# Linear attention with a mixture of experts: the last product of a block inverse gets a stationary operand of 128 columns in place of 64

## The chip, the cores and the metric

The kernel runs on one core of one Trainium2 chip. A core has TensorE (matrix products, from SBUF into PSUM), VectorE, ScalarE and GpSimd (the profile's DVE, ACT and POOL), and SyncE (SP), which here issues most of the transfers. The metric is the device time of one execution in microseconds. The runs of the kernel before have a median of 4116.69 us (4110.34, 4116.69 and 4119.83).

## The reference

The input x is 2 sequences of 2048 tokens with 512 features. It is normalised, and two branches are added to x: a gated delta-rule attention with 16 heads of 128, and a mixture of 16 experts (four per token) on 512 tokens. Cut to what matters, the attention is a recurrence over time with one 128 x 128 state per head:

```python
q, k, v = (silu(conv(x @ W)) for W in (Wq, Wk, Wv))   # k also times DK ** -0.5
for t in range(T):
    err = S @ k[t] - v[t]
    S = alpha[t] * S - beta[t] * outer(err, k[t])
    o[t] = S @ q[t]
out = (layernorm(o) * sigmoid(x @ Wg)) @ Wo
```

## The kernel before, in words

All data are fp32, and an fp32 product stands in the profile as two passes (two MATMUL records and two weight loads, LDWEIGHTS); a transpose is one pass. The kernel does not step through time: it takes chunks of C = 128 tokens. Inside a chunk the recurrence is a triangular system, and its inverse is needed for each head. Heads are taken in pairs (HG = 2), so there are 8 pairs x 2 sequences x 16 chunks = 256 chunk steps. Blocks of four chunks (BLK = 512 tokens) share one projection.

The inverse of a 128 x 128 triangular matrix is put together in steps. GpSimd inverts the diagonal blocks of 32 for a whole pair (`inverses`, L201 to L232). Then, chunk by chunk, `before` (L548 to L616) doubles twice: from 32 to 64 and from 64 to 128. A doubling needs two products in a row, the off-diagonal block times one inverse, then the other inverse times that. Both heads of a pair are handled in one product, since the stationary operands hold the two heads on the diagonal, 64 rows and columns each.

- First doubling: L564 (stationary `a32`, moving `ilo`, 32 columns), a VectorE copy to `xs` (L567), L594 (stationary `ihi`, moving `xs`), from which VectorE makes `iT` (L596) and `top` (L597).
- Second doubling: L605 (stationary `a64`, moving `top[:, 0:64]`, 64 columns, both heads one below the other), a VectorE copy of 64 columns to `xs2` (L607), and L613: stationary `xs2` (128 rows, 64 columns), moving `bot` (128 columns). Its output has 64 rows and, side by side, 64 columns for each head. ScalarE copies it into the upper right part of `inv` (L614).

`after` (L618 to L683) uses it one step later: L633 (stationary `kt`, moving the state S), VectorE makes `r` (L637), L643 (stationary `inv`, moving `r`), ScalarE copies `w` (L646), L652 makes the new state, L666 and L669 the output. `output` transposes it (L699) and stores it.

`recurrence` (L708 on) mixes six ticks of these with work for later: the projections of the next block (`proj`, L151, 512 moving columns, eight passes for one output), the keys and their products for the pair after the next (L151 and L192), the experts (L966, L978, L992), and near the end of each sequence the output projection (L820). So TensorE's queue has wide projection products between the small products of a chunk, and these give the other engines time for the copies in between. On top of this, the framework schedules the recorded program with estimates of its own and sets the order of each engine's queue; a longer copy or a different product can shift it.

Constants come in one transfer at the start (L57): eight 128 x 128 matrices side by side, one of which (`K_ROW`) only holds the row number. `route` uses one column of it (L912 and L916). [...] the small products of `before` use three in turn (tag `l`, always a whole bank).

Of the kernel before, what the change touches and what calls it, by code (L numbers as in the profile page):

```python
# [7 lines left out]
F32 = mybir.dt.float32  # L8
I32 = mybir.dt.int32
AF = mybir.ActivationFunctionType  # L10
ALU = mybir.AluOpType
# [3 lines left out]
P = 128  # L15
NB, T, HID = 2, 2048, 512
H, D, KS = 16, 128, 4
C = 128
# [15 lines left out]
DW = C + 1  # L34


K_ID, K_LE, K_LT, K_GT, K_ONE, K_NEG, K_COL, K_ROW = range(8)
N_CONST = 8


@with_exitstack
def block_kernel(ctx, tc, x, wq, wk, wv, wg, wo, wa, wb, ba, bb, par, consts,
                 topk_idx, topk_w, ew0, ew1, ew2, ewd0, ewd1, out):
    nc = tc.nc
    cp = ctx.enter_context(tc.tile_pool(name="const", bufs=1))
    dp = ctx.enter_context(tc.tile_pool(name="spill", bufs=1, space=DRAM))
    ps_p = ctx.enter_context(tc.tile_pool(name="ps_p", bufs=2, space=PSUM))
    ps_l = ctx.enter_context(tc.tile_pool(name="ps_l", bufs=3, space=PSUM))
# [3 lines left out]
    def bank(pool, tag):  # L52
        return pool.tile([P, 512], F32, tag=tag, name=tag)


    cst = cp.tile([P, N_CONST, P], F32)
    nc.sync.dma_start(out=cst, in_=consts.rearrange("p (n j) -> p n j", j=P))  # L57
    ident = cst[:, K_ID, :]

    def over(m, *dims):  # L60
# [35 lines left out]
    tw = cp.tile([P, FC * TOPK], F32)  # L96
    pos = cp.tile([P, FC * TOPK], I32)

    wrow = cp.tile([P, NT], I32)
    trow = cp.tile([P, NT], I32)  # L100
# [255 lines left out]
    with ExitStack() as es:  # L356
# [135 lines left out]
        mp = es.enter_context(tc.tile_pool(name="moe", bufs=2))  # L492
# [27 lines left out]
        for i, _ in enumerate(f0):  # L520
            next(ot, None)
            next(ot, None)
            if i == 18:
                route(nc, bank, ps_l, mp, cst, topk_idx, topk_w, tw, pos, wrow, trow)
            if i in (24, 26, 28, 30):
                next(p0)
        drain(ot)
# [2 lines left out]
    def bcast(a, n):  # L530
        return bass.AP(a.tensor, a.offset, [*a.ap, (0, n)])

    def v3(t):
        return t.rearrange("p (h j) -> p h j", h=HG)

    HW = HG * D

# [2 lines left out]
    k2 = ctx.enter_context(tc.tile_pool(name="chunk", bufs=2, reuse_waits="tile"))  # L540
# [7 lines left out]
    def before(n, c):  # L548

        u, blk = blocks[n]  # L550
        b = u // NP
        hs = slice((u % NP) * HG, (u % NP) * HG + HG)
        decs, kt, op, qt, _, vs, _ = have[n]
        ci, cs = blk * CB + c, slice(c * C, (c + 1) * C)

        inv = invs[(n * CB + c) % len(invs)]
        for g in range(2):
            nc.sync.dma_start(
                out=inv[g * Q:(g + 1) * Q, :, g * Q:(g + 1) * Q],
                in_=X_d[u][1, :, g, ci, :].rearrange("h (j i) -> j h i", i=Q))  # L560


        px = bank(ps_l, "l")
        nc.tensor.matmul(px[:, 0:Q], lhsT=op["a32"][:, c, :], rhs=op["ilo"][:, c, :],  # L564
                         start=True, stop=True)
        xs = k2.tile([P, Q], F32, tag="xs", name="xs")
        nc.vector.tensor_copy(xs, px[:, 0:Q])  # L567

        pk = bank(ps_l, "l")
        for h in range(HG):  # L570
            nc.tensor.matmul(pk[:, h * C:(h + 1) * C], lhsT=kt[:, h, cs], rhs=qt[:, h, cs],  # L571
                             start=True, stop=True)
        pT = k2.tile([P, HG, C], F32, tag="pT", name="pT", bufs=3)
        for h in range(HG):
            nc.vector.scalar_tensor_tensor(
                pT[:, h, :], pk[:, h * C:(h + 1) * C], D ** -0.5, decs[h][:, c, 1:],
                ALU.mult, ALU.mult)
        yield

        pkv = bank(ps_l, "l")  # L580
        for h in range(HG):
            nc.tensor.transpose(pkv[:, h * D:(h + 1) * D], kt[:, h, cs], ident)
            nc.tensor.transpose(pkv[:, HW + h * D:HW + (h + 1) * D], vs[h][:, cs], ident)  # L583
        kv = k2.tile([P, 2, HG, D], F32, tag="kv", name="kv")
        nc.scalar.copy(kv.rearrange("p s h j -> p (s h j)"), pkv)  # L585
        kg = k2.tile([P, HG, D], F32, tag="kg", name="kg", bufs=3)
        nc.gpsimd.tensor_tensor(kg, kv[:, 0], bcast(gd1[b][:, ci, hs], D), ALU.mult)  # L587
        mark["kg"] = kg[:, 0, 0:1]
        yield
        top, bot = op["top"][:, c, :], op["bot"][:, c, :]  # L590


        pz = bank(ps_l, "l")
        nc.tensor.matmul(pz[:, 0:Q], lhsT=op["ihi"][:, c, :], rhs=xs, start=True, stop=True)  # L594
        iT = k2.tile([P, Q], F32, tag="iT", name="iT")
        nc.vector.transpose(iT, pz[:, 0:Q])  # L596
        nc.vector.scalar_tensor_tensor(  # L597
            top[:, 0:Q], pz[:, 0:Q], second[:, 0:1], top[:, 2 * Q:], ALU.mult, ALU.add)
        for h in range(HG):
            r = 64 * h  # L600
            nc.scalar.copy(bot[r:r + Q, r + Q:r + 2 * Q], iT[r:r + Q])
            nc.gpsimd.tensor_copy(inv[0:Q, h, Q:2 * Q], iT[r + Q:r + 2 * Q])  # L602
        yield
        px = bank(ps_l, "l")
        nc.tensor.matmul(px[:, 0:64], lhsT=op["a64"][:, c, :], rhs=top[:, 0:64], start=True, stop=True)  # L605
        xs = k2.tile([P, 64], F32, tag="xs2", name="xs2")
        nc.vector.tensor_copy(xs, px[:, 0:64])  # L607
        for h in range(HG):
            r = slice(64 * h, 64 * h + 64)
            nc.scalar.copy(inv[64:C, h, 64:C], bot[r, r])  # L610
        yield
        pz = bank(ps_l, "l")
        nc.tensor.matmul(pz[0:64, 0:C], lhsT=xs, rhs=bot, start=True, stop=True)  # L613
        nc.scalar.copy(inv[0:64, :, 64:C], v3(pz[0:64, 0:C]))  # L614
        yield
        found[n, c] = (pT, kv, kg, inv)  # L616

    def after(n, c):  # L618
# [23 lines left out]
        for h in range(HG):  # L642
            nc.tensor.matmul(pw[:, h * D:(h + 1) * D], lhsT=inv[:, h, :], rhs=r[:, h, :],  # L643
                             start=True, stop=True)
        w = k2.tile([P, HG, D], F32, tag="w", name="w")
        nc.scalar.copy(w, v3(pw[:, 0:HW]))  # L646
        mark["w"] = w[:, 0, 0:1]
        yield
# [6 lines left out]
        if S is None:  # L655
            nc.vector.tensor_copy(S2, v3(pss[:, 0:HW]))
        else:
            for h in range(HG):
                nc.vector.scalar_tensor_tensor(
                    S2[:, h, :], S[:, h, :], gtot[b][:, ci, h0 + h:h0 + h + 1],  # L660
                    pss[:, h * D:(h + 1) * D], ALU.mult, ALU.add)
# [46 lines left out]
    def recurrence(b, first):  # L708
# [20 lines left out]
        inv = None  # L729
        for m, at in enumerate([*steps, None, None]):  # L730
            a = before(*at) if at else none
            z = after(*steps[m - 1]) if 0 < m <= len(steps) else none
            y = output(*steps[m - 2]) if m > 1 else none
# [110 lines left out]
    recurrence(1, first)  # L844


def route(nc, bank, ps, mp, cst, topk_idx, topk_w, tw, pos, wrow, trow):

# [2 lines left out]
    n = FC * TOPK  # L853

    def small(tag, cols, dt=F32):
        return mp.tile([P, cols], dt, tag=tag, name=tag, bufs=1)
# [3 lines left out]
                      in_=topk_idx.rearrange("(c p) k -> p c k", p=P))  # L860
    nc.sync.dma_start(out=tw.rearrange("p (c k) -> p c k", c=FC),
                      in_=topk_w.rearrange("(c p) k -> p c k", p=P))
# [11 lines left out]
    for i in range(1, n):  # L874
        nc.tensor.matmul(pr[:, i * NE:n * NE], lhsT=cst[:, K_ONE, :], rhs=sel[:, 0:(n - i) * NE],
                         start=False, stop=i == n - 1)
    pc = bank(ps, "l")
    for i in range(n):
        nc.tensor.matmul(pc[:, 0:NE], lhsT=cst[:, K_ONE, :], rhs=sel[:, i * NE:(i + 1) * NE],
                         start=i == 0, stop=i == n - 1)  # L880
# [26 lines left out]
    te = small("te", NT)  # L907
# [1 line left out]
    for e in range(NE):  # L909
        nc.vector.scalar_tensor_tensor(te, cst[:, K_COL, 0:NT], ends[:, e:e + 1], te, ALU.is_ge, ALU.add)  # L910
    nc.vector.tensor_scalar(te, te, float(NE - 1), float(P), ALU.min, ALU.mult)
    nc.vector.tensor_scalar(te, te, cst[:, K_ROW, 0:1], None, ALU.add)  # L912
    nc.vector.tensor_copy(wrow, te)
    tokf = small("tokf", FC)
    for c in range(FC):
        nc.vector.tensor_scalar(tokf[:, c:c + 1], cst[:, K_ROW, 0:1], float(c * P), None, ALU.add)  # L916


    first = small("first", NT + 1)
# [82 lines left out]
def _constants():  # L1002
    import numpy as np

    i = np.arange(P)
    row, col = i[:, None], i[None, :]
    m = np.zeros((N_CONST, P, P), np.float32)
    m[K_ID] = row == col
    m[K_LE] = row <= col
    m[K_LT] = row < col  # L1010
    m[K_GT] = row > col
    m[K_ONE] = 1.0
    m[K_COL] = col
    m[K_ROW] = row
    m[K_NEG] = np.where(row <= col, 0.0, -1e30)
    return np.ascontiguousarray(m.transpose(1, 0, 2)).reshape(P, N_CONST * P)


def _expert_weights(f):
# [40 lines left out]
```

## Time and profile before

| | |
|---|---|
| median of 3 runs | 4116.69 us |
| profiled execution | 4114.8 us |
| its span, from the first to the last instruction | 4113.0 us |
| mean granted TensorE clock | 0.985 |
| TensorE busy / its weight loads | 3961.7 / 2523.9 us |
| VectorE / ScalarE / GpSimd busy | 2299.5 / 1629.9 / 1841.5 us |
| moved by DMA | 553.79 MB, mean 135 GB/s |

The profile lists one execution. "PE" is TensorE's products, "PEld" its weight loads, which lie beside them. In a group of instructions one reads the line, the engine, the operation, the names of output and inputs, the rows and columns of the stationary operand for TensorE ("128*64"), the shapes and the count; then the busy time in us, the mean duration of one in ns, and the idle time just before them with what ended it. Products on TensorE are pipelined: a record lasts longer than the distance to the next one's start, and the ends are modelled, so distances between starts tell what a product takes. The granted clock is below full in parts of the first 300 us and between the two sequences, where the page's row falls to 8 tenths at the start, and at 9 tenths or more otherwise.

### The profile page before, as it was taken

How to read it: one execution, taken by the hardware profiler on the slowest of the kernel's cores; microseconds unless marked ns; L12 is line 12 of the kernel's file. 1: busy time of each engine (PE TensorE's matmuls, PEld its weight loads, DVE VectorE, ACT ScalarE, POOL GpSimd, SP SyncE). 2: the span in 40 equal slices, each digit the busy share in tenths (PEclk: the TensorE clock that was granted, in tenths of full speed). 3: DMA queues.
4: the chain of work that ended last, by engine and by line, in shares of the span. 5: the costliest groups of instructions: out<-in, count | busy, mean ns of one | idle time of the engine just before them, and what ended most of it. 6: DMA issues, size and time to landing. Idle time of an engine off the chain costs nothing.

```text
span 4113.0 us, 60869 instructions
## 1 busy us (share of the span) xinstructions
PE 3961.7 (96%) x18684; PEld 2523.9 (61%) x18684; DVE 2299.5 (56%) x6621; ACT 1629.9 (40%) x3805; POOL 1841.5 (45%) x3704
## 2 busy tenths in 40 slices
PE   7889999999999999999999899999999999999999
PEld 6755666666666666666664356666666666666554
DVE  6644555555554556666663136666666666666321
ACT  3543333333433434444443224444444444444210
POOL 2373645556464553645451026364545445472110
PEclk8989999999999999999999999999999999999999
DMA  5544454555455454344558733343333333424322
GB/s 187 191 163 136 146 159 148 163 147 165 133 158 150 146 171 114 113 117 132 146 166 266 227 105 110 104 121 95 114 95 109 103 101 107 116 75 118 98 94 77
DMA packets 594738, 553.79 MB, mean 135 GB/s; under 512 B 356016, under 2 KB 422448, under 8 KB 589296
## 3 DMA queue, kind: packets, MB, share of 16 engines
q1 hardware_dynamic: 572304, 468.50, 38.8%
q0 software_dynamic: 22112, 81.41, 6.9%
q8 instruction: 152, 2.49, 0.3%
q14 instruction: 170, 1.39, 0.1%
HBM read 376.27 MB, written 173.41 MB: 134 GB/s over the span
## 4 chain that ended last, share of the span: by engine, by line
PE 73%; DVE 7%; DMA 4%; POOL 3%; ACT 2%; issue 1%; SPq 1%; DVEq 0%; POOLq 0%; ACTq 0%
PE p L151 37%; PE p L820 7%; PE p L978 4%; DVE cv L139 3%; PE c L652 3%; PE l L571 3%; PE c L643 3%; PE o L666 2%; PE p L192 2%; PE c L633 2%; PE o L669 2%; PE l L613 2%; PE p L992 2%; DMA row<-rows_d 2%; DMA out<-xf 1%
## 5 line engine op out<-in xcount | busy, mean ns | idle before, releaser
L139 DVE SCALAR_TENSOR_TENSOR cv<-raw,prm,cv 128x512 f32<-128x512 f32 x1152 | 912.7, 792 | 371.1 <-ACT cv L137 356.8
L151 PE MATMUL p<-xT,wv 128*128 128x512 f32 x1024 | 493.2, 611 | 5.6 <-DVE xgT L968 5.5
L133 ACT COPY raw<-p 128x512 f32<-128x512 f32 x384 | 223.6, 582 | 678.9 <-PE p L151 658.2
L151 PE MATMUL p<-xT,wq 128*128 128x512 f32 x1024 | 481.1, 599 | 0.7 <-DVE xgT L968 0.7
L151 PE MATMUL p<-xT,wg 128*128 128x512 f32 x1024 | 479.5, 601 | 0.2 <-DVE xgT L968 0.2
L820 PE MATMUL p<-wo,oTf 128*128 128x512 f32 x1024 | 464.9, 606 | 13.4 <-DMA oTf<-oT_d 8.3
L151 PE MATMUL p<-xT,wk 128*128 128x512 f32 x896 | 415.9, 603 | 0.3 <-DVE xgT L968 0.2
L820 PEld LDWEIGHTS p<-wo,oTf 128*128 128x128 f32 x1024 | 193.5, 194 | 239.2 <-issue 228.5
L694 DVE TENSOR_SCALAR o<-o,mv,rs 128x128 f32<-128x128 f32 x512 | 187.1, 406 | 238.8 <-POOL rs L680 238.7
L587 POOL TENSOR_TENSOR kg<-kv,gd 128x256 f32<-128x256 f32 x256 | 189.2, 739 | 287.3 <-ACT kv L585 279.9
L602 POOL COPY inv<-iT 32x32 f32<-32x32 f32 x512 | 139.4, 272 | 383.7 <-DVE top L597 251.5
L137 ACT ACTIVATE cv<-p,prm 128x512 f32<-128x512 f32 x384 | 300.9, 784 | 0.0
L220 POOL TENSOR_TENSOR t<-Y 128x30 f32<-128x30 f32 (+14 forms) x480 | 281.0, 585 | 36.8
L151 PEld LDWEIGHTS p<-xT,wv 128*128 128x128 f32 x1024 | 178.9, 191 | 171.9 <-issue 163.8
L223 POOL TENSOR_TENSOR Y<-Y,t 128x30 f32<-128x30 f32 (+14 forms) x480 | 263.9, 550 | 36.6
L151 PEld LDWEIGHTS p<-xT,wg 128*128 128x128 f32 x1024 | 179.4, 190 | 164.1 <-issue 163.7
L680 POOL TENSOR_TENSOR rs<-rs,mhalf 128x2 f32<-128x2 f32 x256 | 184.9, 722 | 212.4 <-DVE rs L679 202.0
L135 POOL COPY halo<-raw 128x3 f32<-128x3 f32 x288 | 76.9, 267 | 430.4 <-ACT raw L133 411.6
L151 PEld LDWEIGHTS p<-xT,wq 128*128 128x128 f32 x1024 | 179.5, 192 | 145.9 <-issue 144.5
L596 DVE STREAM_TRANSPOSE iT<-l 128x32 f32<-128x32 f32 x256 | 55.4, 216 | 375.7 <-PE l L594 375.5
L151 PEld LDWEIGHTS p<-xT,wk 128*128 128x128 f32 x896 | 163.3, 194 | 155.9 <-issue 155.1
L585 ACT COPY kv<-l 128x512 f32<-128x512 f32 x256 | 149.9, 586 | 180.0 <-PE l L583 158.9
(182 smaller groups left out, 7541.9 us busy)
## 6 DMA issues: line engine op xcount, KB each, us to landing
dec_d<-dec SPq DMA_DIRECT2D x128, 258.0 KB
decA<-dec_d SPq DMA_DIRECT2D x128, 258.0 KB
decB<-dec_d SPq DMA_DIRECT2D x128, 258.0 KB
k_d<-kf SPq DMA_DIRECT2D x128, 256.0 KB
k<-k_d SPq DMA_DIRECT2D x64, 512.0 KB
gin<-rows_d SPq DMA_DIRECT2D x128, 256.0 KB
aT_d<-aTf SPq DMA_DIRECT2D x128, 256.0 KB
oT_d<-oT SPq DMA_DIRECT2D x256, 128.0 KB
```

The lines of the kernel that those rows point to most:

```text
L133: nc.scalar.copy(raw[:, KS - 1:], ps)
L137: nc.scalar.activation(cv, ps, AF.Identity, bias=cbias(p, h0 + h), scale=tap(p, h0 + h, KS - 1))
L139: nc.vector.scalar_tensor_tensor(cv, raw[:, j:j + BLK], tap(p, h0 + h, j), cv, ALU.mult, ALU.add)
L151: nc.tensor.matmul(ps, lhsT=w[:, k, h * D:(h + 1) * D], rhs=xt[k], start=(k == 0), stop=(k == NKT - 1))
L220: nc.gpsimd.tensor_tensor(t, bass.AP(col.tensor, col.offset, [col.ap[0], (Q, j), (0, n)]), bass.AP(row.tensor, row.offset, [row.ap[0], (0, ...
L223: nc.gpsimd.tensor_tensor(Y[:, 0:j, j + 1:], Y[:, 0:j, j + 1:], t, ALU.add)
L585: nc.scalar.copy(kv.rearrange("p s h j -> p (s h j)"), pkv)
L587: nc.gpsimd.tensor_tensor(kg, kv[:, 0], bcast(gd1[b][:, ci, hs], D), ALU.mult)
L680: nc.gpsimd.tensor_tensor(rs, rs, mhalf[:, 0:HG], ALU.pow)
L694: nc.vector.tensor_scalar(o[:, h, :], po[:, h * D:(h + 1) * D], mv[:, h, 0:1], rs[:, h:h + 1], ALU.subtract, ALU.mult)
L820: nc.tensor.matmul(py, lhsT=oT[:, h, :], rhs=wos[h], start=(h == 0), stop=(h == H - 1))
L978: nc.tensor.matmul(ps[:fn, s, :], lhsT=w[f][:, s, k, :], rhs=xt[:, k, :], start=(k == 0), stop=(k == NKT - 1))
```

## The change

L605 gets the same 64 columns twice as its moving operand, through an access pattern that repeats them with a step of 0 (`wide`), so its output and the copy `xs2` have 128 columns, the second half equal to the first. L613 then has a stationary operand of 128 columns and writes 128 rows of its bank. The lower 64 are a copy of the upper 64, and nobody reads them: L614 is unchanged.

The wider `xs2` (two buffers, 256 bytes more each) takes 512 bytes more on every partition. The constants take 508 bytes less: the matrix `K_ROW` goes and its one used column is appended, 897 columns in place of 1024.

```diff
-K_ID, K_LE, K_LT, K_GT, K_ONE, K_NEG, K_COL, K_ROW = range(8)
-N_CONST = 8
+K_ID, K_LE, K_LT, K_GT, K_ONE, K_NEG, K_COL = range(7)
+N_CONST = 7
...
-    cst = cp.tile([P, N_CONST, P], F32)
-    nc.sync.dma_start(out=cst, in_=consts.rearrange("p (n j) -> p n j", j=P))
+    cstf = cp.tile([P, N_CONST * P + 1], F32)
+    nc.sync.dma_start(out=cstf, in_=consts)
+    cst = cstf[:, 0:N_CONST * P].rearrange("p (n j) -> p n j", j=P)
...
+    def wide(a):
+
+        n = a.ap[1][1]
+        return bass.AP(a.tensor, a.offset, [a.ap[0], (0, C // n), a.ap[1]])
...
-        nc.tensor.matmul(px[:, 0:64], lhsT=op["a64"][:, c, :], rhs=top[:, 0:64], start=True, stop=True)
-        xs = k2.tile([P, 64], F32, tag="xs2", name="xs2")
-        nc.vector.tensor_copy(xs, px[:, 0:64])
+        nc.tensor.matmul(px[:, 0:C], lhsT=op["a64"][:, c, :], rhs=wide(top[:, 0:64]), start=True, stop=True)
+        xs = k2.tile([P, C], F32, tag="xs2", name="xs2")
+        nc.vector.tensor_copy(xs, px[:, 0:C])
...
-        nc.tensor.matmul(pz[0:64, 0:C], lhsT=xs, rhs=bot, start=True, stop=True)
+        nc.tensor.matmul(pz[:, 0:C], lhsT=xs, rhs=bot, start=True, stop=True)
         nc.scalar.copy(inv[0:64, :, 64:C], v3(pz[0:64, 0:C]))
...
-    nc.vector.tensor_scalar(te, te, cst[:, K_ROW, 0:1], None, ALU.add)
+    nc.vector.tensor_scalar(te, te, number, None, ALU.add)
...
-        nc.vector.tensor_scalar(tokf[:, c:c + 1], cst[:, K_ROW, 0:1], float(c * P), None, ALU.add)
+        nc.vector.tensor_scalar(tokf[:, c:c + 1], number, float(c * P), None, ALU.add)
```

More of the change, by code (lines that the diff above doesn't have):

```diff
@@ L523, in block_kernel @@
             if i == 18:
-                route(nc, bank, ps_l, mp, cst, topk_idx, topk_w, tw, pos, wrow, trow)
+                route(nc, bank, ps_l, mp, cst, cstf[:, N_CONST * P:], topk_idx, topk_w, tw, pos, wrow, trow)
             if i in (24, 26, 28, 30):
@@ L844, in block_kernel, with route @@
     recurrence(1, first)
-def route(nc, bank, ps, mp, cst, topk_idx, topk_w, tw, pos, wrow, trow):
+def route(nc, bank, ps, mp, cst, number, topk_idx, topk_w, tw, pos, wrow, trow):
     n = FC * TOPK
@@ L1013, in _constants @@
     m[K_COL] = col
-    m[K_ROW] = row
     m[K_NEG] = np.where(row <= col, 0.0, -1e30)
-    return np.ascontiguousarray(m.transpose(1, 0, 2)).reshape(P, N_CONST * P)
+    return np.concatenate([m.transpose(1, 0, 2).reshape(P, N_CONST * P), row], axis=1).astype(np.float32)
 def _expert_weights(f):
```

## The prediction

> **What bounds the kernel now.** I read the page's busy shares first, then the chain that ended last, then the waits of TensorE, and then TensorE's timeline in one chunk.
>
> ```profile
> PE 3961.7 (96%) x18684; PEld 2523.9 (61%) x18684; DVE 2299.5 (56%) x6621; ACT 1629.9 (40%) x3805; POOL 1841.5 (45%) x3704
> ...
> PE 73%; DVE 7%; DMA 4%; POOL 3%; ACT 2%; issue 1%; SPq 1%; DVEq 0%; POOLq 0%; ACTq 0%
> ```
>
> TensorE is busy 96% of the span, no other engine more than 56%, and it holds 73% of the chain. Its waits for others are few:
>
> ```profile
> PE l L375 <- DVE row L383: 16.7, 18, 2.4
> PE c L643 <- DVE r L637: 15.5, 30, 0.8
> PE c L419 <- DVE xn L413: 15.3, 5, 12.8
> ...
> PE c L652 <- ACT w L646: 8.3, 29, 0.5
> ...
> PE l L605 <- DVE top L597: 7.9, 18, 0.4
> ...
> PE l L613 <- DVE xs L607: 6.3, 5, 4.1
> ```
>
> The columns are the total in us, the number of waits, the longest. L375 and L419 run before the recurrences; in the chunks the sums are of the order of 10 us in 4113. So a TensorE slot that goes is time that goes, if nothing takes its place. But "busy" hides something: it counts records whose ends are modelled. What counts is from start to start.
>
> ```profile
> 2006.37 0.61 PE L643 MATMUL c<-r,inv 128*128 128x128 f32 x4
> 2006.81 3.60 PE L151 MATMUL p<-xT,wg 128*128 128x512 f32 x8
> 2010.25 0.30 PE L594 MATMUL l<-xs,ihi 128*128 128x32 f32 x2
> ...
> 2012.03 0.33 PE L605 MATMUL l<-top,a 128*128 128x64 f32 x2
> 2012.20 1.11 PE L192 MATMUL p<-kf 128*128 128x128 f32 x8
> 2013.24 0.43 PE L613 MATMUL l<-bot,xs 128*64 128x128 f32 x2
> 2013.60 3.70 PE L151 MATMUL p<-xT,wg 128*128 128x512 f32 x8
> 2017.14 0.30 PE L564 MATMUL l<-ilo,a 128*128 128x32 f32 x2
> ```
>
> The first column is the start in us; each fp32 matmul stands as two passes, so x2 is one. L643 with its full stationary operand ("128*128") takes 0.44 us for 4 passes, 0.11 each, and L151 behind it 3.44 for 8. L613, alone in the chunk with a stationary operand of 64 columns ("128*64"), takes 0.36 for 2 passes, and the eight L151 passes behind it take 3.54. The eight L192 passes ahead of it take 1.04, where 8 × 0.11 and the 0.06 left from L605 make 0.94.
>
> **The change part by part.**
>
> *L613 becomes a full-width product.* From the single records' starts (the timeline rounds them), medians over the 256 chunks:
> - the last pass ahead of L613 to L613: 203 to 205 ns after a 128-column pass, 522 after a 512-column one, where other pairs of such forms have 111 and 429: +93;
> - L613's two passes: 160 apart, against 111: +49;
> - L613 to the next: 203, against 112: +91;
> - the first pass behind it to that one's second: 535 on a 512-column matmul against 429, 132 against 28 on L564: +105.
>
> Together 338 ns a chunk. Weight loads are not prefetched there: the load of L613 starts with its matmul, not some 110 ns ahead as elsewhere. The Trainium skill (TensorEngine Tiling, Key Properties) says that a change of tiling mode drains TensorE, and names no price; 338 ns is the price here. That only 64 columns switch, and not any narrower operand, is seen in L978: its 96-column passes follow 128-column ones, and the reverse, 109 ns apart. After the change no operand of 64 columns or fewer is left, so both switches of a chunk go: 256 × 0.338 = 86.5 us.
>
> Two rules of the skill speak against it. TensorE: Matmul & The Clock Gate, LDWEIGHTS, makes a load's time proportional to its columns, about P/1.2 ns. The wider load then costs 53 ns more, twice a chunk, 256 × 0.107 = 27 us if it is exposed. The rows agree on the size (134 ns for L613, 192 for L571), but L643's passes start 0.11 us apart with such loads, so it is hidden beside the pass ahead. I take 0; by the rule the sum would be 27 us worse. And Tiling's Column Tiling recommends the 64-column mode for such an operand, up to twice as fast: that needs a second product in the other half, and here L613 runs alone between full-width ones, so I take nothing for it.
>
> ```profile
> L613 PE MATMUL l<-bot,xs 128*64 128x128 f32 x512 | 110.5, 297 | 7.7 <-DVE xs L607 6.3 <-ACT bot L601 0.7 <-DVE mv L677 0.6
> ...
> L605 PE MATMUL l<-top,a 128*128 128x64 f32 x512 | 87.4, 252 | 8.0 <-DVE top L597 7.9
> ...
> L978 PE MATMUL p<-xgT,w 128*96 128x128 f32 x496 | 61.4, 275 | 0.0
> ```
>
> *L605 goes from 64 to 128 moving columns.* Its passes start 58 ns apart, the next matmul 111 later, and that one's second pass comes 54 to 58 late, since weight loads of 128 columns keep a cadence of 111: 225 in all. Two 128-column passes (the last two of L643) take 111, 111 and then 4: 226. The columns fill a slot that the loads leave empty: 0 us.
>
> *They are 64 columns read twice,* a step of 0 in the moving operand, of which the trace has no row. Below 0 it can't be. The nearest is L375, whose stationary operand is one column repeated 128 times: its load takes 192 ns, as L571's plain one. I take 0. If the repeat halved the rate, a pass would take 222 and a chunk 0.22 us more: 57 us.
>
> *The copy L607 doubles.*
>
> ```profile
> L607 DVE COPY xs<-l 128x64 f32<-128x64 f32 x256 | 55.0, 215 | 46.2 <-PE l L605 45.9
> L567 DVE COPY xs<-l 128x32 f32<-128x32 f32 x256 | 47.1, 184 | 179.6 <-PE l L564 179.5
> ```
>
> 32 more columns cost 31 ns, 64 more 62: 16 us on a VectorE that is 56% busy, hidden beside TensorE unless L613 waits for it. Without the drain L613's load is wanted some 205 ns earlier (94 of its slot and 111 of prefetch), and the copy ends 62 later. In the trace the copy's end lies 605 ns ahead of that load in the median and never under 52, which is the signal's way. So a chunk is short where it now has under 52 + 267 = 320 ns: 23 of 256 chunks, by 3.9 us in all. There everything behind L613 in TensorE's queue (a projection's L151 or L564) waits with it. Where another VectorE job stands ahead of the copy, that is already in these slacks.
>
> *L613 writes 128 rows of its bank, not 64;* L614 reads the same 64. ScalarE's 234.6 us of waiting for L613 only come earlier. Banks are the same.
>
> *Constants:* the load at the start is 459 KB in place of 524, and the row number is a column of it (same forms in the routing). The first transposes, L419, wait for VectorE's xn, not for it: 0.
>
> *Order.* In the built programs 10,049 of 10,241 TensorE instructions keep their place, and one moves by over 20; VectorE, ScalarE and POOL move as little. Of SP's 3,475 DMA issues 58 move by over 5 places, most around the output stage between the batches and the decay stores. TensorE's only waits for a DMA of note are 8.3 us there; I allow ±5 and take 0.
>
> *What takes the place of the gain.* A wait swallows it only where L613 lies between a product and its consumer. Of the waits above 60 ns on TensorE four do so (L633, L192, L978), so I take 2 us.
>
> **Sum.** 86.5 − 3.9 − 2 = 80.6 us. The profiled execution took 4114.8 us with a span of 4113.0; 1.8 lie outside and stay. It becomes 4034.2. The median of the runs lies 1.9 above it: 4036.
>
> **The rivals.**
> - *Part of the price stays or is taken up.* Were the late second pass behind L613 (105 ns) not the switch's, or as much lost to other waits: 256 × 0.233 − 5.9 = 54 us, 4063. For it: that term is seen only on the pass after. Against: no other matmul with 128 columns ahead of a 512-column one shows it (4 ns after L643).
> - *The repeated operand reads at half rate:* 80.6 − 57 = 24 us, 4093.
> - *The change doesn't do what it says:* what drains is not the width. Then 4117. The 96-column rows and the loads' missing prefetch speak against it.
> - *Slower: the repeat costs far more.* It decides from 269 ns a pass (111 + half of the 315 ns a chunk that are gained). At four times the time a column, a pass takes 429, a chunk 0.64 us more, 163 us: 4199. It needs a restart of the stream at each repeat; nothing in the trace speaks for it.
>
> **How the numbers follow.** The sum 0.87, part stays 0.05, half rate 0.03, no effect 0.02, slower 0.03. Faster by over 0.2% (8 us, about what this kernel's runs can tell) in the first three: 0.95; same 0.02; slower 0.03. The likeliest runs from the lowest run less the whole 86.5, 4024, to 4048, with three times the losses I count. Two in ten may lie outside, and I reach to 4060 for more waits than I see.
>
> **What would show it.** L613 as 128*128, 111 ns from the pass ahead and to the next; eight L151 passes behind it at 3.44 us; L605's passes 111 apart; L607 near 276 ns; TensorE's waits for xs at L613 up from 6.3 to some 10 us. Wrong it would be if L605's passes were further apart than 111, or if the waits for r, w and top in the list grew by tens of us.

## The result, and the profile after

The changed kernel takes 4088.03 us in the median of six runs (4083.15 to 4095.88), the kernel before 4116.36 (4108.26 to 4120.89). The ratio is 0.9939 with a 95% interval of 0.9928 to 0.9949: 28 us faster, where 80 were forecast, and outside the stated range of 4024 to 4060. The profiled execution has a span of 4087.2 us at a granted clock of 0.985.

The page's busy shares and its chain by engine, for the changed kernel:

```profile
PE 3898.7 (95%) x18684; PEld 2542.8 (62%) x18684; DVE 2337.5 (57%) x6621; ACT 1631.5 (40%) x3805; POOL 1822.8 (45%) x3704
...
PE 71%; DVE 10%; DMA 4%; ACT 3%; POOL 2%; issue 1%; SPq 0%; DVEq 0%; ACTq 0%; POOLq 0%
```

TensorE's busy time fell by 63 us, the span by 26. VectorE gained 38 us of busy time and 3 points of the chain; the wider copy explains 18 of the 38, and cv, an instruction of the convolution (L140), another 16. Line numbers behind the change are higher by 6 (L613 is L619, L605 is L611, L607 is L613, L643 is L649, L637 is L643); the lines ahead of it, such as L139 and L151, by 1.

TensorE's timeline of the changed kernel, in the stretch that answers to the one shown of before (start and duration in us):

```profile
1993.82 0.61 PE L649 MATMUL c<-r,inv 128*128 128x128 f32 x4
1994.27 3.60 PE L152 MATMUL p<-xT,wg 128*128 128x512 f32 x8
1997.70 0.30 PE L600 MATMUL l<-xs,ihi 128*128 128x32 f32 x2
...
1999.48 0.39 PE L611 MATMUL l<-top,a 128*128 128x128 f32 x2
1999.71 1.06 PE L193 MATMUL p<-kf 128*128 128x128 f32 x8
2000.60 0.39 PE L619 MATMUL l<-bot,xs 128*128 128x128 f32 x2
2000.82 3.60 PE L152 MATMUL p<-xT,wg 128*128 128x512 f32 x8
2004.26 0.30 PE L570 MATMUL l<-ilo,a 128*128 128x32 f32 x2
```

This is what was forecast. L619 takes 0.22 us in place of 0.36, the eight passes behind it 3.44 in place of 3.54, the eight ahead of it 0.89 in place of 1.04, and L611 with twice the columns 0.23 where the 0.06 late pass behind it is gone. From the first of these lines to the last it is 10.44 us, where it was 10.77.

So the gain is there, and it is lost elsewhere. TensorE's waits (total in us, number, longest) show where:

```profile
PE c L649 <- DVE r L643: 30.9, 41, 0.9
...
PE l L619 <- DVE xs L613: 11.9, 8, 3.9
...
PE c L658 <- ACT w L652: 6.4, 27, 0.5
```

The wait for r, the input of L643, doubled, from 15.5 to 30.9. To see it chunk by chunk I took the distance between the starts of L613 (L619) in successive chunks from the records, 255 steps in each kernel, and subtracted before from after. The table has the mean over eight head pairs that repeat each other closely (5, 6 and 8 to 13; pairs and chunks are counted from 0), away from the experts and the stage between the sequences. "Other twelve" is the sum of the other steps.

| us, after less before | 8 to 9 | 9 to 10 | 12 to 13 | 13 to 14 | other twelve | pair |
|---|---|---|---|---|---|---|
| measured | +0.50 | +0.41 | +0.63 | +0.36 | -3.29 | -1.38 |
| forecast of the switches alone | -0.34 | -0.34 | -0.34 | -0.34 | -4.06 | -5.41 |

Twelve steps keep 3.29 of their 4.06 us (four of them all of it, to 0.01; two, 3 to 4 and 7 to 8, only 0.06 and 0.12). Four got longer, so a pair loses 4.03 us. All four got longer in nine of the 16 pairs (5, 6 and 8 to 14), in pair 7 only the first two. By the profiled executions the pairs 5 to 14 lost 42 us, the rest of the kernel 20; by the medians of the runs it is 58 of the 86.5 in all. What follows is about these ten pairs; the other 20 us are not taken apart.

### The profile page after: what moved, and what is told of

Read it like the earlier page. It is cut to its first block, busy times and chain, and to the rows that moved or that the text cites. A ratio compares the mean times of both kernels' runs of the same rounds, so it can differ in the third digit from the quotient of the medians.

```text
span 4087.2 us, 60899 instructions
## 1 busy us (share of the span) xinstructions
PE 3898.7 (95%) x18684; PEld 2542.8 (62%) x18684; DVE 2337.5 (57%) x6621; ACT 1631.5 (40%) x3805; POOL 1822.8 (45%) x3704
## 4 chain that ended last, share of the span: by engine, by line
PE 71%; DVE 10%; DMA 4%; ACT 3%; POOL 2%; issue 1%; SPq 0%; DVEq 0%; ACTq 0%; POOLq 0%
PE p L152 35%; PE p L826 8%; DVE cv L140 4%; PE p L984 3%; PE c L658 3%; PE c L649 3%; PE l L577 3%; PE p L193 2%; PE o L672 2%; PE c L639 2%; PE o L675 2%; DMA row<-rows_d 2%; PE p L998 2%; PE l L619 1%; DVE rs L685 1%
## 5 line engine op out<-in xcount | busy, mean ns | idle before, releaser
L140 DVE SCALAR_TENSOR_TENSOR cv<-raw,prm,cv 128x512 f32<-128x512 f32 x1152 | 928.7, 806 | 362.4 <-ACT cv L138 347.7
L152 PE MATMUL p<-xT,wv 128*128 128x512 f32 x1024 | 476.0, 596 | 5.6 <-DVE xgT L974 5.5
L593 POOL TENSOR_TENSOR kg<-kv,gd 128x256 f32<-128x256 f32 x256 | 172.4, 673 | 275.7 <-ACT kv L591 269.2
L224 POOL TENSOR_TENSOR Y<-Y,t 128x30 f32<-128x30 f32 (+14 forms) x480 | 274.8, 572 | 36.5
L221 POOL TENSOR_TENSOR t<-Y 128x30 f32<-128x30 f32 (+14 forms) x480 | 272.2, 567 | 36.8
L649 PEld LDWEIGHTS c<-r,inv 128*128 128x128 f32 x960 | 137.2, 192 | 150.9 <-issue 61.3
```

The source lines that it names most:

```text
L140: nc.vector.scalar_tensor_tensor(cv, raw[:, j:j + BLK], tap(p, h0 + h, j), cv, ALU.mult, ALU.add)
L152: nc.tensor.matmul(ps, lhsT=w[:, k, h * D:(h + 1) * D], rhs=xt[k], start=(k == 0), stop=(k == NKT - 1))
L221: nc.gpsimd.tensor_tensor(t, bass.AP(col.tensor, col.offset, [col.ap[0], (Q, j), (0, n)]), bass.AP(row.tensor, row.offset, [row.ap[0], (0, ...
L224: nc.gpsimd.tensor_tensor(Y[:, 0:j, j + 1:], Y[:, 0:j, j + 1:], t, ALU.add)
```

## What happens in the four steps

The first of them, in pair 10. VectorE's timeline in the kernel before:

```profile
2935.65 0.35 DVE L637 SCALAR_TENSOR_TENSOR r<-c,gd,kv 128x128 f32<-128x128 f32 x1
2935.90 0.75 DVE L139 SCALAR_TENSOR_TENSOR cv<-raw,prm,cv 128x512 f32<-128x512 f32 x1
2936.56 0.35 DVE L637 SCALAR_TENSOR_TENSOR r<-c,gd,kv 128x128 f32<-128x128 f32 x1
```

and GpSimd's:

```profile
2936.11 1.01 POOL L587 TENSOR_TENSOR kg<-kv,gd 128x256 f32<-128x256 f32 x1 [0.22 <-ACT kv L585]
```

The same two in the changed kernel:

```profile
2919.39 0.34 DVE L643 SCALAR_TENSOR_TENSOR r<-c,gd,kv 128x128 f32<-128x128 f32 x1
2919.65 1.11 DVE L140 SCALAR_TENSOR_TENSOR cv<-raw,prm,cv 128x512 f32<-128x512 f32 x1
2920.68 0.34 DVE L643 SCALAR_TENSOR_TENSOR r<-c,gd,kv 128x128 f32<-128x128 f32 x1
```

```profile
2919.59 0.61 POOL L593 TENSOR_TENSOR kg<-kv,gd 128x256 f32<-128x256 f32 x1
```

Here cv is a step of the convolution for later work, kg the keys of a chunk times their decay. In VectorE's queue a cv stands between the two halves of r (one per head), and L643's second half waits for the second r. So cv is on the path here. In the kernel before it starts 0.21 us ahead of kg, takes 0.75, and kg takes 1.01. In the changed kernel kg starts 0.06 ahead of cv, takes 0.61, and cv takes 1.11. Kg's input, kv, comes by way of TensorE's transposes and ScalarE, which are now earlier; r comes by way of VectorE's queue, which is not. The Trainium skill (SBUF — State Buffer, Who interferes with whom) has the rule that fits: VectorE and GpSimd share a pair of ports, for which an instruction of VectorE with two SBUF inputs, such as cv, contends with one of GpSimd that reads SBUF, such as kg; the first to start holds it to its end. The rows agree: kg ends at 2920.20, and cv ends 0.56 later.

My theory from here: (1) the switches cost 0.34 us a chunk, as forecast; (2) in four steps of each pair TensorE was not the bound. A chain runs through VectorE's queue, from L594 over top, S, cv, the copy, the statistics, o and pT to r, and back to TensorE at L643's second half; L613 lies beside it, so its 0.34 us there only become waiting; (3) kg overtaking cv, the wider copy and the shifted order make this chain longer. The rivals: the new order of the queues takes it all, or the wider copy does.

The rows of the same step in the kernel before show such a chain, with one link that the theory has wrong. In them q is the activation of the finished convolution, qg that q times its decay, rs the scale for normalising o. TensorE's lines, then VectorE's, then ScalarE's and GpSimd's:

```profile
2927.65 0.30 PE L594 MATMUL l<-xs,ihi 128*128 128x32 f32 x2
...
2930.60 0.43 PE L613 MATMUL l<-bot,xs 128*64 128x128 f32 x2
...
2936.09 0.46 PE L643 MATMUL c<-r,inv 128*128 128x128 f32 x2
2937.06 0.46 PE L643 MATMUL c<-r,inv 128*128 128x128 f32 x2 [0.51 <-DVE r L637]
```

```profile
2927.99 0.22 DVE L596 STREAM_TRANSPOSE iT<-l 128x32 f32<-128x32 f32 x1 [2.50 <-PE l L594]
...
2929.15 0.84 DVE L139 SCALAR_TENSOR_TENSOR cv<-raw,prm,cv 128x512 f32<-128x512 f32 x1
2929.91 0.21 DVE L607 COPY xs<-l 128x64 f32<-128x64 f32 x1
2930.05 0.73 DVE L139 SCALAR_TENSOR_TENSOR cv<-raw,prm,cv 128x512 f32<-128x512 f32 x1
...
2930.92 0.74 DVE L139 SCALAR_TENSOR_TENSOR cv<-raw,prm,cv 128x512 f32<-128x512 f32 x1
...
2932.52 1.17 DVE L679 TENSOR_SCALAR rs<-mv 128x2 f32<-128x2 f32 x1
2934.51 0.73 DVE L694 TENSOR_SCALAR o<-o,mv,rs 128x128 f32<-128x128 f32 x2 [0.82 <-POOL rs L680]
2935.15 0.18 DVE L567 COPY xs<-l 128x32 f32<-128x32 f32 x1
2935.25 0.48 DVE L575 SCALAR_TENSOR_TENSOR pT<-l,decB 128x128 f32<-128x128 f32 x2
```

```profile
2931.69 0.63 ACT L141 ACTIVATE q<-cv 128x512 f32<-128x512 f32 x1 [0.36 <-DVE cv L139]
```

```profile
2932.40 1.26 POOL L319 TENSOR_TENSOR qg<-q,gin 128x512 f32<-128x512 f32 x1 [0.40 <-ACT q L141]
2933.77 0.71 POOL L680 TENSOR_TENSOR rs<-rs,mhalf 128x2 f32<-128x2 f32 x1
```

VectorE starts when L594 ends, ahead of L613. Its third cv ends at 2931.66; ScalarE's q starts 0.03 us later, GpSimd's qg 0.08 behind q, GpSimd's rs 0.11 behind qg, and VectorE's o 0.03 behind that. From o VectorE works without a stop to r. The same distances (to 0.06 us) stand in all four steps, in the medians of the eight pairs, before and after the change. So between cv and o the link is not the statistics on VectorE, as the theory has it, but ScalarE's q and GpSimd's qg and rs: 2.85 us. VectorE's own rs, of two columns, is held up until qg ends, beside this chain.

## The experiments

**The copy and the order without the wide product.**

```diff
-        nc.tensor.matmul(pz[:, 0:C], lhsT=xs, rhs=bot, start=True, stop=True)
+        nc.tensor.matmul(pz[0:64, 0:C], lhsT=xs[:, 0:64], rhs=bot, start=True, stop=True)
```

> L605 and the copy are 128 columns wide as in the change, but L613 takes only the first 64 columns of the copy as its stationary operand and writes 64 rows again. Its queues hold the same instructions in the same order as the changed kernel's. Theory (the switches cost 86 us; the gain is lost in four chunks of each head pair that a chain through VectorE bounds, where GpSimd's kg now starts ahead of VectorE's cv and stretches it): the switches are back and TensorE is as late as before, so kg follows cv again; only the copy's 62 to 74 ns are added in those 64 chunks, 5 us: 4116 to 4126. Rival (the new order of the queues costs the 60 us): before plus 60, about 4176. Rival (the wider copy costs them): about 4176 too.

Measured: 4135.26 us (4131.43 to 4138.87), ratio to before 1.0043 (1.0030 to 1.0057). It is 19 us above before: more than my theory had (at most 10), far less than the rivals' 60. The switches are back, and nine of the other twelve steps are as in the kernel before to 0.01 us. The group of L619 in this run:

```profile
L619 PE MATMUL l<-bot,xs 128*64 128x128 f32 x512 | 110.3, 297 | 15.1 <-DVE xs L613 12.6 <-ACT q L142 1.4 <-ACT inv L616 0.9
```

Against the changed kernel, with the same queues in the same order, the width of the product is worth 47 us. The four steps are longer than before by 0.16, 0.11, 0.64 and 0.12. The 0.64 is the order. TensorE's timeline in that step, kernel before:

```profile
2977.54 0.38 PE L643 MATMUL c<-r,inv 128*128 128x128 f32 x2
2977.76 1.02 PE L151 MATMUL p<-xT,wq 128*128 128x512 f32 x2
2978.62 0.38 PE L643 MATMUL c<-r,inv 128*128 128x128 f32 x2
2978.84 1.02 PE L151 MATMUL p<-xT,wq 128*128 128x512 f32 x2
```

and this run:

```profile
2997.38 0.38 PE L649 MATMUL c<-r,inv 128*128 128x128 f32 x2
2998.19 0.46 PE L649 MATMUL c<-r,inv 128*128 128x128 f32 x2 [0.43 <-DVE r L643]
2998.49 1.88 PE L152 MATMUL p<-xT,wq 128*128 128x512 f32 x4
```

Before, one projection matmul of 0.86 us stood between L643's halves and filled the wait for r. One place in the order, and TensorE stands still instead.

**The wide product without the copy and the order.** The upper half of the stationary operand is zeros: `xs2` is now a list of two fixed tiles that are set to 0 once, ahead of the chunks.

```diff
-        nc.tensor.matmul(px[:, 0:C], lhsT=op["a64"][:, c, :], rhs=wide(top[:, 0:64]), start=True, stop=True)
-        xs = k2.tile([P, C], F32, tag="xs2", name="xs2")
-        nc.vector.tensor_copy(xs, px[:, 0:C])
+        nc.tensor.matmul(px[:, 0:64], lhsT=op["a64"][:, c, :], rhs=top[:, 0:64], start=True, stop=True)
+        xs = xs2[(n * CB + c) % 2]
+        nc.vector.tensor_copy(xs[:, 0:64], px[:, 0:64])
```

> L613 is 128 columns wide, but the upper 64 columns of its stationary operand are zeros written once (two fixed buffers); L605 and the copy stay at 64 columns, and the queues of TensorE, VectorE and ScalarE hold the order of the kernel before. Theory (VectorE's chain and the port it shares with GpSimd in four chunks of a pair): the switches are gone, the loss remains but for the copy's 0.07 us in 64 chunks: 4076 to 4086. Rival (the new order) and rival (the wider copy): both causes are gone, so the whole gain is seen, about 4034.

Measured: 4073.19 us (4071.24 to 4075.82), 0.9893 (0.9878 to 0.9908). TensorE, VectorE and ScalarE have the order of the kernel before and the copy takes 64 columns, yet only 43 of 86 us are gained: neither rival takes it all. What they take together is the 15 us between this run and the changed kernel. The four steps: +0.35, +0.33, 0.00, +0.36. The cv between the halves of r grew by as much: from 0.74 to 1.11, from 0.74 to 1.08, not at all (0.84), and from 0.74 to 1.10 (medians of the eight pairs). A cv between the halves of r that takes over 0.9 us occurs in 2 chunks of the kernel before, in 30 of the changed one, in 2 of the run before this and in 30 of this one. It follows the switches, not the order or the copy.

**Kg taken from GpSimd,** on the changed kernel and on the kernel before.

```diff
-        nc.gpsimd.tensor_tensor(kg, kv[:, 0], bcast(gd1[b][:, ci, hs], D), ALU.mult)
+        for h in range(HG):
+            j = hs.start + h
+            nc.scalar.activation(kg[:, h, :], pkv[:, h * D:(h + 1) * D], AF.Identity, scale=gd1[b][:, ci, j:j + 1])
```

> The changed kernel with kg made by two ScalarE activations from PSUM in place of one GpSimd product. Theory (shared port, kg against cv): in the four chunks of a pair cv between the two halves of r is back at 0.75 us and the second half of r starts 0.92 us after the first, in place of 1.3; 64 x 0.4 = 25 us less, about 4062. If kg is not what stretches cv: cv stays near 1.1 there, and the time is 4088 or above it, for ScalarE has some 0.6 us more in each chunk.

> The kernel before with kg on ScalarE as in the run e3. Theory (shared port): in the kernel before cv starts ahead of kg in the four chunks and is not stretched by it, so little changes: 4105 to 4125, and e3 then stands some 50 us below this run. If GpSimd's load as such slows VectorE all through: some 25 us less here too, about 4090.

Measured: 4069.69 us (4063.89 to 4070.48), 0.9882 (0.9867 to 0.9897), and 4113.19 (4105.94 to 4118.18), 0.9990 (0.9982 to 0.9999). The forecasts were 4062 and no change. The four steps of the first, against before: +0.02, +0.11, +0.55, +0.12, where the changed kernel has +0.50, +0.41, +0.63, +0.36. A cv over 0.9 us between the halves is left in 2 chunks, and in none of the second. So kg on GpSimd is what stretched cv; that they meet at the port is the skill's rule, which the starts and ends above fit. The first stands 8 us higher than forecast: the four steps give back 1.10 us a pair, where I had put 0.4 into each, and the step from 12 to 13, whose cv had not grown, hardly moves. ScalarE's work also costs something (two of the other steps go from -0.34 to +0.18), and the other twelve together end 0.25 worse. Cv as a whole, in the changed kernel and in the first of these runs:

```profile
L140 DVE SCALAR_TENSOR_TENSOR cv<-raw,prm,cv 128x512 f32<-128x512 f32 x1152 | 928.7, 806 | 362.4 <-ACT cv L138 347.7 <-POOL inv L608 0.4 <-ACT bot L607 0.2
```

```profile
L140 DVE SCALAR_TENSOR_TENSOR cv<-raw,prm,cv 128x512 f32<-128x512 f32 x1152 | 888.9, 772 | 368.0 <-ACT cv L138 349.5 <-ACT q L142 3.0 <-POOL inv L610 0.4
```

The mean falls from 806 to 772 ns; before the change it was 792.

**Cv taken out of the chain.** The halves of r get a higher priority with the scheduler, and no cv stands between them in any chunk. Three kernels: the changed one, the one before, and the one with zeros in the upper half.

```diff
-            for h in range(HG):
+            with tc.high_priority():
+                for h in range(HG):
                     nc.vector.scalar_tensor_tensor(
                         r[:, h, :], pq[:, h * D:(h + 1) * D], gd0[b][:, ci, h0 + h:h0 + h + 1],
                         kv[:, 1, h, :], ALU.mult, ALU.add)
```

> The changed kernel with a higher scheduling priority for the two halves of r, so that no cv stands between them in VectorE's queue in any chunk (before: in 85 of 240). Theory (a chain through VectorE, from L594 over top, S, the copy, statistics and r to the second half of L643, bounds four chunks of each pair, and cv between the halves of r is a link of it): the chain is some 0.66 us shorter and the stretched cv is out of it; those chunks fall by about 1.0 us against the changed kernel, 40 to 64 of them: 4024 to 4048. If VectorE's chain is not what bounds them: 4088 as the changed kernel.

> The kernel before with the same priority for r. Theory: TensorE's waits of about 0.67 us at the second half of L643 go, in 40 or more chunks: 25 us, about 4090; those chunks are then bound by TensorE, and the change on top of it (run e6) is worth nearly its 86 us less what other waits take: 45 to 65. If VectorE's chain doesn't bound them: 4116, and e6 at 4088.

> The zeros in the upper half of the stationary operand (run e2) with r's halves together. Theory: narrow copy, the order of the kernel before, and the short chain: 4020 to 4040, 5 to 15 below e6. If what e2 has over the changed kernel is not the order and the copy, no less than e6.

| kernel | us (lowest to highest) | ratio to before (95%) |
|---|---|---|
| changed, r together | 4048.73 (4046.83 to 4055.50) | 0.9839 (0.9823 to 0.9856) |
| before, r together | 4093.05 (4087.78 to 4099.77) | 0.9941 (0.9923 to 0.9959) |
| zeros, r together | 4039.28 (4033.20 to 4040.58) | 0.9806 (0.9790 to 0.9822) |

The product behind r, in the run with zeros without the priority and with it:

```profile
L650 PE MATMUL c<-r,inv 128*128 128x128 f32 x960 | 165.0, 286 | 52.3 <-DVE r L644 25.7 <-issue 10.1 <-POOL t L221 4.6
```

```profile
L651 PE MATMUL c<-r,inv 128*128 128x128 f32 x960 | 154.7, 283 | 19.6 <-POOL Y L224 8.0 <-issue 4.4 <-POOL t L221 2.2
```

The 19.6 us that are left are put down to others, but in each of the four steps L651 starts 0.10 us behind the end of the first half of r: what is left is mostly still a wait for r, now for its first half.

The place of r in VectorE's queue is worth 24 us to the kernel before and 39 to the changed one: it was the bound in these chunks. Not all of it comes from there. The priority also takes r ahead of other work (in chunks 3, 7 and 11 it starts 1.4 to 2.8 us sooner behind L633) and moves L613 in chunk 12, so the steps from 11 to 13 must be read together. Of 2.60 us a pair that the kernel before gains, the four steps have 1.59; of 4.03 in the changed one, 3.27. The width, which was worth 28 us, is now worth 44 (54 with the narrow copy), just under the 45 to 65 that I had expected; the changed kernel itself ends just above its 4024 to 4048. And what is left shows the second point of the theory at its cleanest. With r together, zeros less before:

| us | 8 to 9 | 9 to 10 | 12 to 13 | 13 to 14 | other twelve | pair |
|---|---|---|---|---|---|---|
| zeros less before, r together | +0.01 | 0.00 | 0.00 | 0.00 | -3.43 | -3.42 |
| changed less before, r together | +0.01 | +0.11 | +0.11 | +0.11 | -3.13 | -2.80 |

The queues of TensorE, VectorE and ScalarE are the same in the first row, and TensorE has 0.34 us less to do in every step. In four steps this makes no difference at all: ahead of L643 TensorE waits there 0.26 to 0.35 us longer. Without the wide product it waits in only one of the four, so in the other three its work and r end almost together. The second row adds the wide copy and the changed order: 0.11 in three of these steps, where the copy's own excess is 0.07.

**Kg besides.**

> Run e7 with kg on ScalarE besides. Theory: cv is no link of the chain any more, so a cv stretched by kg costs nothing there: within 10 us of e7. If GpSimd's kg slows VectorE's chain elsewhere too: 10 us or more below e7.

Measured: 4036.89 us (4030.77 to 4041.19), 0.9803 (0.9787 to 0.9820). Within 10 us of the run without, as expected: with cv out from between the halves of r, stretching it costs nothing that the total shows. The steps do move: kg on ScalarE costs 0.52 in each of two others, and the one from 8 to 9 gains 0.53, for which no run here shows the cause.

**One link less for VectorE.** The run with zeros and r together, with the copy ahead of L613 on ScalarE (`nc.scalar.copy` in place of `nc.vector.tensor_copy`).

> Run e7 with the copy ahead of L613 on ScalarE, so one link of 0.21 us leaves VectorE's chain and TensorE's work stays as it is. Theory (VectorE's chain still bounds the four chunks of a pair in e7, which took 0.00 us less than in e9 though TensorE had 0.34 less to do): those chunks fall by about 0.2 us, 40 to 64 of them, 8 to 13 us in all: 4026 to 4032, if ScalarE's queue doesn't bring the copy late elsewhere. If another engine bounds them: 4039 as e7 or above.

Measured: 4033.77 us (4028.53 to 4039.79), 0.9802 (0.9786 to 0.9819), 5.5 us below its base, with ranges that overlap, and above the 4026 to 4032 that the theory asked for. The total decides nothing. The four steps change by -0.20, -0.29, -0.07 and -0.28: they react to work taken from the other engines' path, where 0.34 us of TensorE left them at 0. The other twelve got longer by 2.02 in sum, so the eight pairs lose; the lower total comes from the pairs that run beside the experts. The size of the reaction is not the copy's alone: the order of VectorE's queue shifted too, and GpSimd's rs comes 0.14 us sooner after qg.

The run also shows which link sets the pace ahead of o. VectorE's lines, then GpSimd's, in the step from 8 to 9 of pair 10:

```profile
2878.48 0.17 DVE L687 TENSOR_SCALAR rs<-mv 128x2 f32<-128x2 f32 x1
2880.47 0.73 DVE L702 TENSOR_SCALAR o<-o,mv,rs 128x128 f32<-128x128 f32 x2 [1.82 <-POOL rs L688]
```

```profile
2878.49 1.28 POOL L320 TENSOR_TENSOR qg<-q,gin 128x512 f32<-128x512 f32 x1 [0.40 <-ACT q L142]
2879.74 0.70 POOL L688 TENSOR_TENSOR rs<-rs,mhalf 128x2 f32<-128x2 f32 x1
```

VectorE's rs starts just ahead of qg and takes 0.17 us in place of 1.17, and o waits 1.82 in place of 0.82: it still starts when GpSimd's rs ends. So the chain goes over qg and GpSimd's rs, and the statistics are beside it. What it would give to take qg from GpSimd, no run here shows.

## Why the prediction was wrong

**Right, to the size.** The price of the two switches: 338 ns a chunk, which shows as -0.34 us in the steps where TensorE waits for nothing. L605 with 128 columns at no cost, its passes 111 ns apart; the repeated moving operand at full rate (no difference from a plain one, so the half-rate rival falls); the wider weight load hidden. By the Trainium skill's rule on load times (TensorE: Matmul & The Clock Gate, LDWEIGHTS) an estimate would have asked 27 us more, and the passes at 111 ns show none of it. The copy takes 285 ns (forecast 276), and the waits for it at L613 grew from 6.3 to 11.9 us (forecast some 10).

**The step that failed is "What takes the place of the gain", at 2 us.** In all 58 us went, where I had counted 5.9. I looked for waits with L613 between a product and its consumer. The product that r reads, L633, comes behind L613, so by that test the wait of L643 for r did not count. It was the wrong test. The r that L643 waited for was late because of a chain that starts at L594, ahead of L613, and runs over VectorE's cv, ScalarE's q and GpSimd's qg and rs back to VectorE. A saving beside such a chain is worth nothing. Part of the evidence was on the page: "PE c L643 <- DVE r L637: 15.5, 30" was the second in my own list, and I summed it away as some 10 us in 4113. Such waits are only what sticks out of an almost balanced chain; they say which chunks are bound elsewhere, not how much is lost by it. By the profile of before one could have said: these 30 waits lie, all but two, in three of the four steps of ten pairs; such chunks don't gain, and 30 x 0.34 = 10 us go. The fourth step, 12 to 13, has no wait there, but L643 has a reserve of only 0.25 us behind r, less than the 0.34. The prediction's own sign of being wrong, that the waits for r grow by tens of us, was near: they grew by 15.

**"Order: take 0" failed too.** That 10,049 of 10,241 instructions keep their place is no measure. One matmul that moved by one place costs 0.64 us in each of nine pairs, some 6 us in all.

**"Hidden on a VectorE that is 56% busy" was wrong in those chunks.** The copy's excess was priced only against L613's own wait for it. In the four steps it is a link of the chain.

**Not foreseen: kg overtaking cv.** I treated the engines beside TensorE as unchanged. A faster TensorE brings kv earlier, GpSimd starts sooner, and the cv between the halves of r takes 0.23 to 0.36 us longer in three of the four steps.

The account for one pair of the eight, in us: 5.41 forecast; 1.36 that four steps could not give; 1.90 by which they grew (1.04 in the run with only the wide product, which is kg; 1.03 in the run with only copy and order; together 0.17 less than their sum); 0.77 that the other twelve did not give; 1.38 left. Of the 0.77, 0.50 lies in the steps from 3 to 4 and from 7 to 8; with kg on ScalarE in both kernels the change has most of it back there (-0.33 and -0.26), but the cause stays open, as it does for the pairs outside the ten. The rival "part of the price stays or is taken up" had the right direction with 4063, but not the mechanism.

**The best version** here has zeros in the upper half in place of a repeated operand, and r's halves together: 4039.28 us, and 4036.89 and 4033.77 with kg or the copy on ScalarE, which the runs don't tell apart. All three beat both kernels.

## What to carry to other kernels

A saving on the busiest engine is worth nothing in the stretches where it already waits, however small its waits are in sum, and little where its reserve is smaller than the saving. Cut the loop into steps and look in each for the wait that ends last. Follow it back through the other engine's queue to where that queue last stood idle, and from there to the engine that ended the stop, not to the last product that it needs. A product of 64 stationary columns among 128-column ones pays for two switches; pad it with zeros that are written once, and no copy gets longer. After an edit that shifts the order, compare which instruction now stands between a wait and what used to fill it.

## What the runs showed of the hardware

The switch to a 64-column stationary operand and back costs 93 + 49 + 91 + 105 = 338 ns in a stream of fp32 passes, and the last 105 fall on the second pass after the return. A 96-column operand costs nothing of it (109 ns to or from a 128-column one). A step of 0 in the moving operand costs nothing (111 ns a pass).

VectorE's cv and GpSimd's kg take turns: the first to start keeps its 0.75 or 0.61 us, and the other takes 1.11 or 1.01. It reaches the smallest instruction. VectorE's rs, of two columns, takes 169 ns in the median of the kernel before and 170 in the changed one, but over 0.9 us in 46 and 53 of the 256 chunks. In the changed kernel, for one (VectorE's line, then GpSimd's):

```profile
2916.26 1.17 DVE L685 TENSOR_SCALAR rs<-mv 128x2 f32<-128x2 f32 x1
```

```profile
2916.14 1.26 POOL L320 TENSOR_TENSOR qg<-q,gin 128x512 f32<-128x512 f32 x1 [0.40 <-ACT q L142]
```

It starts 0.12 us behind a GpSimd product of 512 columns and ends 0.03 behind its end.
